# First group of the two 16-head pipelines taken in parts of 1, 1 and 2 tiles

## The chip, the cores and the metric

The kernel runs on one core of one Trainium2 chip. The metric is device time of one launch in microseconds (us): the median of repeated runs. A separate profiled execution gives the trace.

## The reference

A four-layer network with gated cross-attention and mixture-of-experts blocks on `x` of shape (2, 1024, 256), so N = 2048 tokens of 256 numbers, with a context of 64 rows per batch. Everything is float32. Each layer adds two blocks to `x`, each on a layer norm of `x` without learned scale:

```python
x = x + tanh(g_xattn[l]) * xattn_l(layernorm(x), ctx)
x = x + tanh(g_ffn[l])   * ffn_l(layernorm(x))
```

The attention of layers 1 and 3, which the change is about, has 16 heads of width 16 over the 64 context rows of the token's batch:

```python
q, k, v = (split_heads(t @ W + b) for ...)          # queries from x, keys and values from ctx
scores  = einsum('bhqd,bhkd->bhqk', q, k) / sqrt(16)
scores  = where(mask, scores, -1e9)
out     = einsum('bhqk,bhkd->bhqd', softmax(scores), v) @ Wo + bo
```

Layer 0 uses linear attention and a routed feed-forward, layer 2 a single-head attention, layer 1 a dense sum over all eight gated experts, layers 0, 2 and 3 route tokens to experts (one expert per token in layers 0 and 2, two in layer 3, with a capacity in 2 and 3).

## The kernel before

**Tiling.** The residual `x` stays in SBUF as `xs`, 16 tiles of 128 tokens (NT = 16), handled in four groups of four tiles (TG = 4, GW = 512 tokens). Context keys and values of a 16-head layer are turned once into block-diagonal operands `kblk` and `vblk` (`Heads.setup`), so that scores of 16 heads and 64 keys are eight matrix products per tile.

**Stages in order.** Layer 0 attention; layer 0 experts (`moe0`), whose outputs are added by indirect DMA into a copy of the residual in DRAM (`xd`); at its end `heads1.setup` and `xattn2_setup` prepare layers 1 and 2, and `reload(xd)` brings the residual back, one DMA of 512 KB for each group, on SP's queue. Then `middle`: the layer-1 pipeline, the dense experts of layer 1 and the attention of layer 2. Then the experts of layer 2 (`moe_capacity`), which end with `heads3.setup` and another `reload`. Then `last_attention`, the layer-3 pipeline, with the routing of layer 3; then its experts.

**A pipeline.** `Heads.pipeline` walks the 16 tiles. At step i it issues the transposes of the probabilities of tile i-1 (`turned`), the scores and softmax of tile i (`scores`), the products with `vblk` and the division for tile i-1 (`quotients`), and the output product for tile i-2 (`output`), which adds the result to `xs`. Between these it advances two lists of generators: `coming`, which prepares the next group, and `gone`, which norms finished groups for the next block. What a group needs before its scores is made by `ready(g)`: `norm_steps` takes statistics of all four tiles (`stats`, line 203: two VectorE operations per tile, then a handful of operations on 4 elements per partition, with Ln and Exp on ScalarE), normalises two tiles on ScalarE and two on GpSimd (lines 248 and 253), transposes the group with eight TensorE operations (line 271) and copies it out of PSUM on ScalarE (line 179); `query_steps` (line 511) forms the queries of all 512 tokens in two accumulations of two products (line 279), adds the bias on ScalarE (line 517), and adds the gated output bias to the group's rows of `xs` in one GpSimd operation of 128x1024 (line 524). Group 0 runs through all of it first: `run(ready(0))` stands ahead of the loop.

The mask enters the scores as a product that starts the accumulation (line 542); the eight score products are line 548. In layer 1 the softmax subtracts the maximum on VectorE (lines 568 and 569) and takes one exponential (line 578); in layer 3 half of the heads take it one head at a time with the maximum as bias (lines 561 and 564). Line 590 transposes the probabilities, line 609 is `quotients`' product, lines 621 to 625 its division, line 640 the addition to `xs`.

**What sets the order.** The framework records each instruction with its reads and writes, and schedules them when the program is complete: each engine gets its own list, an instruction is placed where its operands are ready by a cost model, and the program's order is the priority. At run time an engine takes its list strictly in order and waits on semaphores. Dependencies go by the region of a tile that an instruction touches.

**Others that the change touches.** `int_ramp` (line 78) makes integer ramps once at the start and converts them. The weights of layer 1's experts come in by SP's queue behind `reload`, and GpSimd forms sums of weight blocks from them (lines 1329 to 1332) while the pipeline runs.

## Time and profile before

| what | value |
|---|---|
| median of 3 runs | 2223.36 us (2222.18 to 2229.72) |
| the profiled execution | 2234.64 us, its span 2232.9 us |
| mean granted TensorE clock in it | 0.941 |
| PE busy | 2070.0 us, 93% of the span |
| DVE, ACT, POOL busy | 1320.5, 934.0, 1148.6 us (59%, 42%, 51%) |
| layer-1 pipeline: reload issued, first statistics, first scores | 338.48, 342.28, 359.25 us |
| layer-3 pipeline: reload issued, first statistics, first scores | 1910.12, 1914.03, 1928.19 us |

PE stands for TensorE's products, PEld for its loads of the stationary operand, DVE for VectorE, ACT for ScalarE, POOL for GpSimd, SP for the engine whose queue issues most DMAs. "Lnnn" is a line of the kernel. Times in the trace count from the first instruction. The granted clock is the share of full speed that TensorE was given; in the stretches shown it is 0.50 or 1.00. Idle time of an engine is written with what released it.

### The profile page before, as it was taken

How to read it: one execution, taken by the hardware profiler on the slowest of the kernel's cores; microseconds unless marked ns; L12 is line 12 of the kernel's file. 1: busy time of each engine (PE TensorE's matmuls, PEld its weight loads, DVE VectorE, ACT ScalarE, POOL GpSimd, SP SyncE). 2: the span in 40 equal slices, each digit the busy share in tenths (PEclk: the TensorE clock that was granted, in tenths of full speed). 3: DMA queues.
4: the chain of work that ended last, by engine and by line, in shares of the span. 5: the costliest groups of instructions: out<-in, count | busy, mean ns of one | idle time of the engine just before them, and what ended most of it. 6: DMA issues, size and time to landing. Idle time of an engine off the chain costs nothing. (4 is left out here: it accounts for less than half of the span.)

```text
span 2232.9 us, 31536 instructions
## 1 busy us (share of the span) xinstructions
PE 2070.0 (93%) x11296; PEld 1739.8 (78%) x11296; DVE 1320.5 (59%) x2920; ACT 934.0 (42%) x2108; POOL 1148.6 (51%) x1341
## 2 busy tenths in 40 slices
PE   6739998999999999999999999999996999698897
PEld 3339995678888788888788887888885999365797
DVE  5851117766666676566666666666564566577564
ACT  4414443653333333333433334333332555374454
POOL 3225655126666556666366665566660665311673
PEclk8859998999999999999999999999995899797899
DMA  3135542012222232222222222322230354111352
GB/s 102 48 105 182 160 138 97 6 43 90 90 85 85 76 102 88 85 85 91 83 91 85 85 86 76 103 86 86 86 104 29 116 140 125 52 39 58 104 149 58
DMA packets 108532, 201.05 MB, mean 90 GB/s; under 512 B 20052, under 2 KB 47960, under 8 KB 105790
## 3 DMA queue, kind: packets, MB, share of 16 engines
q1 hardware_dynamic: 83144, 162.18, 22.7%
q0 software_dynamic: 19728, 36.03, 6.2%
q8 instruction: 90, 1.47, 0.3%
q10 hardware_dynamic: 5504, 0.82, 0.2%
q14 instruction: 66, 0.54, 0.1%
HBM read 206.89 MB, written 21.91 MB: 102 GB/s over the span
## 5 line engine op out<-in xcount | busy, mean ns | idle before, releaser
L1698 PE MATMUL ps_b<-xsum,w 128*128 128x256 f32 x1536 | 386.7, 381 | 2.6 <-DVE c L1724 2.6
L1329 POOL TENSOR_TENSOR w<-w 128x256 f32<-128x256 f32 x224 | 165.0, 737 | 386.2 <-DMA w<-in_L_Wu_dram 184.1
L1698 PEld LDWEIGHTS ps_b<-xsum,w 128*128 128x128 f32 x1536 | 290.7, 190 | 48.5 <-issue 4.6
L1380 ACT COPY u<-ps_b 128x512 f32<-128x512 f32 (+5 forms) x242 | 118.9, 491 | 435.4 <-PE ps_b L1743 255.9
L1698 PE MATMUL ps_a<-hT,w 128*128 128x256 f32 x1024 | 265.9, 381 | 0.2 <-ACT ps_b L1362 0.2
L1698 PEld LDWEIGHTS ps_a<-hT,w 128*128 128x128 f32 x1024 | 194.4, 191 | 27.2 <-ACT ps_b L1362 0.6
L1332 POOL TENSOR_TENSOR w<-w 128x256 f32<-128x256 f32 x224 | 186.0, 830 | 16.9
L1330 POOL TENSOR_TENSOR w<-w 128x256 f32<-128x256 f32 x224 | 193.6, 864 | 0.0
L1331 POOL TENSOR_TENSOR w<-w 128x256 f32<-128x256 f32 x224 | 192.0, 857 | 0.0
L1362 ACT COPY ps_b<-ps_a 128x512 f32<-128x512 f32 (+5 forms) x242 | 115.4, 477 | 121.0 <-DVE b L1728 70.3
L1368 ACT COPY m<-ps_e 128x512 f32<-128x512 f32 (+5 forms) x242 | 117.9, 488 | 39.0 <-PE ps_e L1743 26.4
L1760 POOL TENSOR_TENSOR m<-m,accT 128x256 f32<-128x256 f32 x60 | 71.7, 1196 | 120.4 <-ACT m L1368 118.3
L1698 PE MATMUL ps_e<-hT,w 128*128 128x256 f32 x512 | 133.1, 381 | 0.4 <-ACT m L1368 0.4
L1698 PE MATMUL ps_e<-xsum,w 128*128 128x256 f32 x512 | 132.9, 380 | 0.0
L1724 DVE TENSOR_TENSOR c<-ps_e,u 128x512 f32<-128x512 f32 x64 | 44.2, 691 | 148.7 <-ACT u L1380 148.7
L1743 PE MATMUL ps_b<-t,w 128*128 128x256 f32 x512 | 132.1, 381 | 0.0
L1743 PE MATMUL ps_a<-b,w 128*128 128x256 f32 x512 | 131.4, 379 | 0.0
L1725 DVE TENSOR_TENSOR b<-b,c 128x512 f32<-128x512 f32 x128 | 118.1, 922 | 4.1
L1698 PEld LDWEIGHTS ps_e<-hT,w 128*128 128x128 f32 x512 | 97.4, 191 | 15.5 <-ACT m L1368 1.8
L1705 ACT ACTIVATE b<-b 128x512 f32<-128x512 f32 x128 | 80.7, 631 | 67.9 <-DVE b L1713 62.6
L1743 PEld LDWEIGHTS ps_b<-t,w 128*128 128x128 f32 x512 | 97.7, 191 | 13.3
L1698 PEld LDWEIGHTS ps_e<-xsum,w 128*128 128x128 f32 x512 | 96.7, 190 | 14.1 <-issue 1.3
(418 smaller groups left out, 4413.1 us busy)
## 6 DMA issues: line engine op xcount, KB each, us to landing
w<-in_L_Wg_dram SPq DMA_DIRECT2D x64, 512.0 KB, 3.8
w<-in_L_Wu_dram SPq DMA_DIRECT2D x64, 512.0 KB, 3.8
w<-in_L_Wd_dram SPq DMA_DIRECT2D x64, 512.0 KB, 3.6
w<-in_L_W_dram SPq DMA_DIRECT2D x64, 512.0 KB, 4.2
hd_L<-h SPq DMA_DIRECT2D x8, 512.0 KB, 3.0
b<-b2d SPq DMA_DIRECT2D x23, 128.0 KB, 4.3
xs<-in_x_dram SPq DMA_DIRECT2D x4, 512.0 KB
xd<-xs SPq DMA_DIRECT2D x4, 512.0 KB, 2.8
```

The source lines that it names most:

```text
L1329: lambda: eng.tensor_add(s[0], a21, a22),
L1330: lambda: eng.tensor_sub(s[1], s[0], a11),
L1331: lambda: eng.tensor_sub(s[2], a11, a21),
L1332: lambda: eng.tensor_sub(s[3], a12, s[1]),
L1362: A.copy(self.b, self.pa)
L1368: A.copy(self.sb5, self.pe)
L1380: A.copy(u2, self.b)
L1698: T.matmul(ps[:, q * 256 : (q + 1) * 256], lhsT=lhs[kind][:, q, :], rhs=xr[kind], start=(first and q == 0), stop=True, skip_group_check=True,)
L1705: done[0] = A.activation(dst, src, AF.Silu)
L1725: V.tensor_mul(m[name], m[name], c)
L1743: T.matmul(ps, lhsT=wd[kind][:, q, :], rhs=m["rhs"][kind][:, q * 256 : (q + 1) * 256], start=(clear and q == 0), stop=True, skip_group_che ...
L1760: G.tensor_add(sb, sb, acc[:, i, j])
```

## The change

Group 0 of both 16-head pipelines is taken in parts of one, one and two tiles.

- `reload` brings group 0 back in three DMAs (128, 128 and 256 KB), groups 1 to 3 in one each as before.
- A new `parts_steps` takes statistics, normalises, transposes and copies out one part at a time. The first tile of a part is normalised on ScalarE, the second on GpSimd: in all three tiles on ScalarE and one on GpSimd. A part of n tiles has 2n transposes into one PSUM tile and one copy.
- `query_steps` is split into `new_queries` and `some_queries`, which forms the queries of the given tiles alone and adds the output bias tile by tile, in operations of 128x256, for all groups.
- `Heads.first` runs group 0: four products of the first loaded tile with itself (128x128 by 256 columns) into a PSUM tile that nobody reads, then the parts.
- `pipeline` starts the first part ahead of the scores of tile 0, the second after them, the third after the scores of tile 1; the transposes of tile 0's probabilities come after that. Later groups are prepared as before.
- `int_ramp` keeps its integers in a work buffer (`w`) rather than in one of its own. `stats` uses tiles cut to its n. The router has a parts variant and a tag argument, which nothing calls or sets.

```diff
     def int_ramp(shape, pattern, base, mult, name):
-        ti = const.tile(shape, I32, name=name + "_i")
+        ti = wpool.tile([P, 2048], F32, name="w")[:, : shape[1]].bitcast(I32)
...
+    def parts_steps(g, parts, psp, hpool, hTpool):
+        xg = xs[:, g * TG : (g + 1) * TG, :]
+        h = hpool.tile([P, TG, D], F32, name="h")
+        hT = hTpool.tile([P, NC, GW], F32, name="hT")
+        yield h, hT
+        for t0, n in parts:
+            mv, rstd = stats(xg[:, t0 : t0 + n], n, True)
+            off = small.tile([P, TG], F32, name="off")[:, :n]
+            V.scalar_tensor_tensor(off, mv[:, :, 0], -1.0, rstd, ALU.mult, ALU.mult)
+            for t in range(n):
+                if t % 2:
+                    G.tensor_scalar(
+                        h[:, t0 + t, :], xg[:, t0 + t, :], rstd[:, t : t + 1],
+                        off[:, t : t + 1], ALU.mult, ALU.add,
+                    )
+                else:
+                    A.activation(
+                        h[:, t0 + t, :], xg[:, t0 + t, :], AF.Identity,
+                        bias=off[:, t : t + 1], scale=rstd[:, t : t + 1],
+                    )
+            yield
+            ps = psp.tile([P, GW], F32, name="ps_tr")
+            for c in range(NC):
+                for t in range(n):
+                    T.transpose(
+                        ps[:, (c * n + t) * P : (c * n + t + 1) * P],
+                        h[:, t0 + t, c * P : (c + 1) * P], ident,
+                    )
+            A.copy(
+                hT[:, :, t0 * P : (t0 + n) * P],
+                ps[:, : NC * n * P].rearrange("p (c q) -> p c q", c=NC),
+            )
+            yield t0, n
...
+        def some_queries(self, g, hT, qT, t0, n, pools):
+            at = slice(t0 * P, (t0 + n) * P)
             for c in range(NC):
-                ps = py.tile([P, 512], F32, name="ps_y")
-                mm256(ps, lambda k: self.wq[:, k, c * P : (c + 1) * P], lambda k: hT[:, k, :])
+                ps = pools["py"].tile([P, 512], F32, name="ps_y")
+                mm256(
+                    ps[:, : n * P], lambda k: self.wq[:, k, c * P : (c + 1) * P],
+                    lambda k: hT[:, k, at],
+                )
                 A.activation(
-                    qT[:, c, :], ps, AF.Identity, bias=cols[:, self.c_bq, c : c + 1]
+                    qT[:, c, at], ps[:, : n * P], AF.Identity,
+                    bias=cols[:, self.c_bq, c : c + 1],
                 )
                 yield
-            self.qT[g] = qT
-
-            xg = xs[:, g * TG : (g + 1) * TG, :]
-            G.tensor_add(xg, xg, self.bo.unsqueeze(1).to_broadcast([P, TG, D]))
+            for t in range(g * TG + t0, g * TG + t0 + n):
+                G.tensor_add(xs[:, t, :], xs[:, t, :], self.bo)
+
+        def first(self, parts, pt, hp, hTp, pools):
+            idle = pools["ps"].tile([P, 512], F32, name="ps_s")
+            for _ in range(4):
+                T.matmul(
+                    idle[:, :D], lhsT=xs[:, 0, :P], rhs=xs[:, 0, :], start=True, stop=True
+                )
+            steps = parts_steps(0, parts, pt, hp, hTp)
+            _, hT = next(steps)
+            qT = self.new_queries(0, pools)
+            for found in steps:
+                if found:
+                    run(self.some_queries(0, hT, qT, *found, pools))
+                    yield
...
-            run(ready(0))
+            begun = ready(0)
...
+                if i == 0:
+                    next(begun)
+                if i > 1 and i - 1 < NT:
                     self.turned(i - 1, pools)
                 if i < NT:
                     self.scores(i, pools)
+                if i <= 1:
+                    next(begun)
+                if i == 1:
+                    self.turned(0, pools)
...
+    PARTS = [(0, 1), (1, 1), (2, 2)]
...
     def reload(xd):
-        for g in range(NG):
+        for a, n in ((0, 1), (1, 1), (2, 2), *((g * TG, TG) for g in range(1, NG))):
             nc.sync.dma_start(
-                residual(g), xd[g * GW : (g + 1) * GW, :].rearrange("(t p) d -> p t d", p=P)
+                xs[:, a : a + n, :],
+                xd[a * P : (a + n) * P, :].rearrange("(t p) d -> p t d", p=P),
             )
...
                 def ready(g):
+                    if g == 0:
+                        return heads1.first(PARTS, pools["pt"], hp, hTp, pools)
+                    return later(g)
```

With `if 0 <= i - 1 < NT` replaced by `if i > 1 and i - 1 < NT`, the step order of tiles from 1 on is as before. The layer-3 `ready` is changed in the same way with `heads3`.

More of the change, by code (lines that the diff above doesn't have):

```diff
@@ L202, in stats @@
     def stats(src, n, by_log=False):
-        st = small.tile([P, TG, 6], F32, name="st")
-        mv = small.tile([P, TG, 2], F32, name="mv")
+        st = small.tile([P, TG, 6], F32, name="st")[:, :n]
+        mv = small.tile([P, TG, 2], F32, name="mv")[:, :n]
         for t in range(n):
@@ L207, in stats @@
             V.bn_aggr(mv[:, t, :], st[:, t, :])
-        ve = small.tile([P, TG], F32, name="ve")
+        ve = small.tile([P, TG], F32, name="ve")[:, :n]
         V.tensor_scalar_add(ve, mv[:, :, 1], EPS)
         if by_log:
-            y = small.tile([P, TG], F32, name="y0")
+            y = small.tile([P, TG], F32, name="y0")[:, :n]
             A.activation(y, ve, AF.Ln)
@@ L215, in stats @@
         else:
-            yi = small.tile([P, TG], I32, name="yi")
+            yi = small.tile([P, TG], I32, name="yi")[:, :n]
             V.tensor_single_scalar(yi, ve.bitcast(I32), 1, ALU.logical_shift_right)
@@ L220, in stats @@
         for i in range(1 if by_log else 3):
-            q = small.tile([P, TG], F32, name="q")
+            q = small.tile([P, TG], F32, name="q")[:, :n]
             V.tensor_mul(q, y, y)
             V.scalar_tensor_tensor(q, q, -0.5, ve, ALU.mult, ALU.mult)
-            rstd = small.tile([P, TG], F32, name=f"rstd{i}")
+            rstd = small.tile([P, TG], F32, name=f"rstd{i}")[:, :n]
             V.scalar_tensor_tensor(rstd, q, 1.5, y, ALU.add, ALU.mult)
@@ L511, in query_steps, with new_queries @@
         def query_steps(self, g, hT, pools):
-            two, py = pools["two"], pools["py"]
-            qT = two.tile([P, NC, GW], F32, name="qT", bufs=pools.get("nq", 1))
-            for c in range(NC):
-                ps = py.tile([P, 512], F32, name="ps_y")
-                mm256(ps, lambda k: self.wq[:, k, c * P : (c + 1) * P], lambda k: hT[:, k, :])
+            yield from self.some_queries(g, hT, self.new_queries(g, pools), 0, TG, pools)
+        def new_queries(self, g, pools):
+            self.qT[g] = pools["two"].tile(
+                [P, NC, GW], F32, name="qT", bufs=pools.get("nq", 1)
+            )
+            return self.qT[g]
+        def some_queries(self, g, hT, qT, t0, n, pools):
+            at = slice(t0 * P, (t0 + n) * P)
+            for c in range(NC):
+                ps = pools["py"].tile([P, 512], F32, name="ps_y")
[3 more added lines that the diff above has]
+                )
                 A.activation(
-                    qT[:, c, :], ps, AF.Identity, bias=cols[:, self.c_bq, c : c + 1]
+                    qT[:, c, at], ps[:, : n * P], AF.Identity,
+                    bias=cols[:, self.c_bq, c : c + 1],
                 )
                 yield
-            self.qT[g] = qT
-            xg = xs[:, g * TG : (g + 1) * TG, :]
-            G.tensor_add(xg, xg, self.bo.unsqueeze(1).to_broadcast([P, TG, D]))
+            for t in range(g * TG + t0, g * TG + t0 + n):
[5 more added lines that the diff above has]
+                    idle[:, :D], lhsT=xs[:, 0, :P], rhs=xs[:, 0, :], start=True, stop=True
+                )
+            steps = parts_steps(0, parts, pt, hp, hTp)
[5 more added lines that the diff above has]
+                    yield
         def scores(self, tt, pools):
@@ L653, in pipeline @@
                 if i < NT and i % TG == 0:
-                    advance(coming, 99)
+                    advance(coming, 999)
                     if i + TG < NT:
                         coming.append(ready(i // TG + 1))
-                if 0 <= i - 1 < NT:
+                if i == 0:
+                    next(begun)
+                if i > 1 and i - 1 < NT:
                     self.turned(i - 1, pools)
@@ L802, in bc, with logit_steps @@
         return ap.unsqueeze(2).to_broadcast([P, ap.shape[1], n])
-    def logit_steps(ps, at, hT, which):
-        for t in range(TG):
+    def logit_steps(ps, at, hT, which, t0=0, n=TG):
+        for t in range(t0, t0 + n):
             mm256(
@@ L812, in logit_steps, with choose_steps @@
                 yield
-    def choose_steps(psp, rp, nt, ps, bias, top, before):
+    def choose_steps(psp, rp, nt, ps, bias, top, before, tag="ps_m"):
         rev = rev8.unsqueeze(1).to_broadcast([P, nt, E])
@@ L850, in choose_steps @@
         W = nt * E
-        pk = psp.tile([P, 512], F32, name="ps_m")
+        pk = psp.tile([P, 512], F32, name=tag)
         T.matmul(pk[:, :W], lhsT=upper_b, rhs=flat, start=True, stop=False)
@@ L857, in choose_steps @@
             )
-        pc = psp.tile([P, 512], F32, name="ps_m")
+        pc = psp.tile([P, 512], F32, name=tag)
         for t in range(nt):
@@ L1243, in group_steps, with parts_steps, slot_steps @@
             yield from self.slot_steps(g * TG, TG, ps, psp, rp)
-        def slot_steps(self, t0, nt, ps, psp, rp):
+        def parts_steps(self, g, parts, pt, psp, hpool, hTpool, rp, tag="ps_m"):
+            steps = parts_steps(g, parts, pt, hpool, hTpool)
+            h, hT = next(steps)
+            lg = rp.tile([P, TG, E], F32, name="r_some")
+            for found in steps:
+                if found:
+                    t0, n = found
+                    ps = psp.tile([P, 512], F32, name=tag)
+                    run(logit_steps(ps, 0, hT, self.which, t0, n))
+                    biased = lg[:, t0 : t0 + n]
+                    at = ps[:, t0 * E : (t0 + n) * E].rearrange("p (t e) -> p t e", e=E)
+                    if self.bias is None:
+                        V.tensor_copy(biased, at)
+                    else:
+                        V.tensor_add(
+                            biased, at, self.bias.unsqueeze(1).to_broadcast([P, n, E])
+                        )
+                yield found
+            self.rows(g, h)
+            yield
+            yield from self.slot_steps(
+                g * TG, TG, lg.rearrange("p t e -> p (t e)"), psp, rp, tag, biased=True
+            )
+        def slot_steps(self, t0, nt, ps, psp, rp, tag="ps_m", biased=False):
             top = self.top
             p1, _, ex, rk = yield from choose_steps(
-                psp, rp, nt, ps, self.bias, top, self.before
+                psp, rp, nt, ps, None if biased else self.bias, top, self.before, tag
             )
@@ L1300, in slot_steps @@
             yield
-            pi = psp.tile([P, 512], F32, name="ps_m")
+            pi = psp.tile([P, 512], F32, name=tag)
             for t in range(n):
@@ L1817, in ready, with later @@
                 def ready(g):
+                    if g == 0:
+                        return heads1.first(PARTS, pools["pt"], hp, hTp, pools)
+                    return later(g)
+                def later(g):
                     _, hT = yield from norm_steps(g, pools["pt"], hp, hTp, by_act=True, halved=True)
@@ L1916, in ready, with later @@
             def ready(g):
+                if g == 0:
+                    return heads3.first(PARTS, pools["pt"], hp, hTp, pools)
+                return later(g)
+            def later(g):
                 _, hT = yield from norm_steps(g, pools["pt"], hp, hTp, by_act=True, halved=True)
```

## The prediction

> **What bounds the kernel now.** First the page: PE is busy for 93% of the span and no other engine for over 59%; its slices of 55.8 us stand mostly at 9; the 8 of the seventh and the 6 of the 35th hold the starts of the two 16-head pipelines. The chain of waits over the whole span is split over hundreds of short pieces, so I went to the two places that the change touches: the start of the layer-1 pipeline (after the reload at 338.5 us) and of the layer-3 pipeline (reload at 1910.1 us). The windows there, cut where the granted clock changes; the columns are the stretch, its length, the busy time of PE, PEld, DVE, ACT and POOL with instruction counts, granted clock, DMA share and GB/s.

> ```profile
> 341.00:349.40 8.40, 6.10 (x24) 4.29 (x23) 3.98 (x19) 0.00 (x0) 0.00 (x0) 0.50 1.07 395
> 349.40:356.20 6.80, 5.41 (x14) 2.67 (x14) 6.76 (x25) 2.80 (x8) 4.71 (x6) 0.50 0.62 245
> 356.20:363.00 6.80, 3.62 (x13) 1.34 (x11) 3.28 (x6) 3.63 (x8) 6.40 (x9) 1.00 0.00 1
> 363.00:366.40 3.40, 3.14 (x13) 1.85 (x13) 2.29 (x4) 0.00 (x0) 3.40 (x5) 0.50 0.00 0
> ...
> 1909.20:1918.70 9.50, 0.00 (x0) 0.00 (x0) 4.67 (x26) 1.12 (x4) 1.18 (x7) 0.50 0.78 275
> 1918.70:1922.90 4.20, 3.98 (x10) 1.93 (x10) 4.13 (x14) 2.08 (x7) 3.40 (x3) 0.50 0.02 5
> 1922.90:1929.70 6.80, 3.99 (x14) 1.78 (x15) 3.65 (x7) 3.30 (x7) 5.70 (x6) 1.00 0.00 0
> 1929.70:1943.40 13.70, 13.70 (x66) 7.85 (x63) 5.23 (x9) 7.66 (x24) 1.42 (x1) 0.50 0.00 1
> ```

> The reader sees two losses: TensorE stands (9.5 us flat in layer 3), and what it does it does mostly at half clock. From 1943.4 and 366.4 on the clock is full and PE is 97% busy (19.40 and 19.61 of 20 us in the windows from 1950 on), so PE's work sets the end of both stages, and what counts is how early that work is done. Then the timeline, for what keeps TensorE waiting (start, length, engine, line, operation, tiles, shapes, count, idle time before and its releaser):

> ```profile
> 342.28 0.43 DVE L206 BATCH_NORM_STATS2 st<-xs 128x6 f32<-128x256 f32 x1 [3.49 <-DMA xs<-xd]
> ...
> 354.60 2.35 POOL L524 TENSOR_TENSOR xs<-xs,bo 128x1024 f32<-128x1024 f32 x1
> 354.70 2.27 DVE L225 SCALAR_TENSOR_TENSOR rstd<-q,y 128x4 f32<-128x4 f32 x1
> ...
> 359.25 0.70 PE L548 MATMUL ps_s<-kblk,qT 64*128 64x256 f32 x4 [0.22 <-ACT qT L517]
> ```

> ```profile
> 1914.03 0.75 DVE L206 BATCH_NORM_STATS2 st<-xs 128x6 f32<-128x256 f32 x2 [5.39 <-DMA xs<-xd_L]
> ...
> 1918.73 2.09 PE L271 MATMUL ps_tr<-ident,h 128*128 128x128 f32 x8 [11.56 <-POOL h L253]
> ...
> 1924.47 2.21 DVE L225 SCALAR_TENSOR_TENSOR rstd<-q,y 128x4 f32<-128x4 f32 x1
> ...
> 1928.19 0.70 PE L548 MATMUL ps_s<-kblk,qT 64*128 64x256 f32 x4 [1.93 <-ACT qT L517]
> ```

> From the landing of group 0 to the first score product 17.0 us pass in layer 1 and 14.2 in layer 3: four tiles of statistics, normalising, eight transposes and the 512-column queries, all before tile 0 gets its scores. Three times (354.70, 1919.54, 1924.47) a 4-element DVE operation of some 0.15 us takes 2.1 to 2.3 us beside the 2.35 us bias add of POOL.

> **The change part by part.** *Reload in six DMAs.* Layer 3 issues at 1910.12 and moves 131 KB in 1911 to 1912 and 276 KB in the next us; the first 512 KB are through at about 1913.3, and DVE starts 0.7 later. The first 128 KB are through at 1912.0: tile 0 lands at about 1912.7, 1.3 us earlier; in layer 1, by its windows in the same way, at 341.0 and not 342.3. Two more issues of 0.5 us each on SP put groups 1 to 3, and the weight loads queued behind them, 1.0 us later; the queue moves 380 to 390 GB/s without a break until 353 and its end is not waited for, so I cost this at nothing; without that cover, 1.0 us.

> *Tile 0 alone.* Its chain from rows of layer 3: statistics 0.40+0.16+0.15 on DVE (0.65 with overlap), two ACT steps 0.6, the four small DVE steps 1.15 with other tiles' statistics between (1916.80 to 1917.95), ACT's normalising 0.65, two transposes at half clock 0.7, the copy of 256 elements 0.5 (512 take 0.59), two 128-column queries 0.6, two bias steps 0.75 (512 take 0.67 each): 5.6 us. Scores could begin at 1912.7+5.6 = 1918.3, not 1928.2. This is not the gain: afterwards PE is the bound.

> *What it is worth at the end.* I count PE's work in us of full clock, busy times clock. Layer 3, landing to 1943.4: 3.98/2 + 3.99 + 13.70/2 = 12.8. Layer 1, from 341.0 to 366.4: 6.10/2 + 5.41/2 + 3.62 + 3.14/2 = 10.9, the layer-2 setup included. The same work has to be done after. The clock steps at 339.1, 356.2, 363.0, 366.4 and at 1909.2, 1922.9, 1929.7, 1943.4, always whole multiples of 3.41 us apart, so the new ramp gets a full clock at one of these edges. [...]

> Layer 3: PE begins real work at about 1916.2 and, with tiles coming singly, is taken to be 80% occupied (between the 59% of 1922.9 to 1929.7 and the full 13.70 after). At half clock until 1929.7 it does 13.5*0.4 = 5.4; the other 7.4 at 95% take 7.8: done at 1937.5, 5.9 us earlier. Full clock one edge sooner (1926.3) gives 7.9, one later (1933.1) 3.9. I take 5.9, because the 13.7 us after 1929.7, transposes and half-row scores at 100% busy, show that this mix does not raise the clock soon. Layer 1: the setup products keep PE at 85%; half clock until 356.2 does 6.5, the rest 4.5 takes 4.7: done at 360.9, 5.5 earlier (7.4 with the edge at 352.8, 3.6 with 359.6).

> *Four unread products.* No row shows one; a 256-column fp32 pass at half clock starts every 0.42 us (1929.85 to 1931.12), so four take 1.7. In layer 3 PE has nothing else (11.56 idle); in layer 1 they stand on its in-order queue with the setup behind them: between -1.7 (the clock rises an edge sooner) and +1.7 a head. I take 0.

> *Bias by tiles.* Sixteen adds a stage at 0.73 (the 128x256 sums) and not four at 2.35: POOL +2.3 us a stage, idle afterwards in layer 3. DVE behind one waits 0.7 and not 2.2; the hits at 354.70, 1919.54 and 1924.47 lie in the stretches counted above, so nothing is added. [...] The first rival has a row that waited longer.

> *The rest.* Eight more query products and loads a head at about 0.1 over the same columns, 0.5 in all on PE at worst for both; ACT gets one more tile and some ten short steps a head, under scores that wait for PE. The ramps in work buffers are read at 9.85 to 10.46, the buffers next written at 24.5: nothing. The parts variant of the router and the new arguments are not called: nothing. `pipeline` turns tile 0 after the scores of tile 1: one exchange, nothing.

> Sum: -5.9-5.5+0.5 = -10.9. The profiled execution took 2234.64 (span 2232.9 and 1.7 around it), so 2223.7 by its own time; the median is 11.3 below that execution, and 2223.4-10.9 = 2212.5. About 0.3%, 6.7 us, is what a measurement of this kernel can tell from no change.

> **The rivals.** *POOL's train takes layer 1's gain back.* POOL runs weight sums almost without a break from 351.5 to 378.8. In that run one operation waited through seven sums:

> ```profile
> 373.29 4.91 DVE L625 SCALAR_TENSOR_TENSOR oT<-rs,oT 128x256 f32<-128x256 f32 x1
> ```

> Tile 0 now reaches L625 some 10 us deeper in the run; if it gets through only at its end, the first output product is no earlier than its 378.3 of now and layer 1 gains nothing: -5.4, 2218. Against it: the other small DVE steps there waited for one sum each. *The clock is raised at once.* If the four products fill enough of a window, layer 3 runs full from 1916.1: 10 us at 80%, the other 4.8 at 95%, done at 1931.3, 12.1 earlier; with layer 1's 7.4 that is -19, 2204. [...] 1.7 us of queries and four transposes sufficed in 1919.5 to 1922.9; 1.9 of mask products did not in 349.4 to 352.8. *The clock stays down (slower).* The pieces are sparser than the dense 512-column queries that raised it at 356.2 and 1922.9; each further edge at half clock costs 3.41/2 = 1.7. It decides from 10.9/1.7, over six edges more than I count in the two ramps together; ten give +6 to +7, 2230. For it: four edges in a row at full occupancy after 1929.7. [...] Against it: group 1's 512-column queries must come within some 20 us. *It does not do what it says:* where the parts are queued in order behind other groups' steps on ACT and DVE, as the normalising of groups 1 and 2 was put ahead of tile 0's scores before, tile 0 is not early: -1, 2222.

> **How the numbers follow.** Forecast 0.55 (its own range 2206 to 2219: an edge sooner or later in both layers gives 2209 to 2216, and the products' bounds some 3 more); POOL's train 0.18; clock at once 0.12; not what it says 0.07; clock down 0.08. Faster: 0.55 + 0.12 + a sixth of the train's 0.18 = 0.70; the train's rest and the 0.07 are same, 0.22; slower 0.08. The range takes in the first three down to the clock-at-once case and up to the fourth, and leaves out the clock-down case and the tails of those two: 2203 to 2222.

> **What would show it.** First statistics within 3 us of the reload's first issue; scores of tile 0 at about 6 us after that landing; PE idle before the first transposes of layer 3 some 2.5 us shorter; the windows from the landing to the steady 97% shorter by 5 to 6 us in each layer, with the clock full for good by about 20 us after the landing; no DVE step of 2.2 us beside a bias add. It is wrong if scores of tile 0 still start over 12 us after the landing, if the first output of layer 1 waits for POOL's last sum, or if the half clock lasts as long as before.

## The result and the profile after

| | before | after |
|---|---|---|
| median of the timed runs | 2224.43 us (2220.96 to 2231.23, 10 runs) | 2212.22 us (2204.32 to 2220.75, 10 runs) |
| ratio (that of the two medians is 0.9945, inside the interval) | | 0.9931, 95% interval 0.9914 to 0.9948 |
| profiled execution, span, mean granted clock | 2234.64, 2232.9 us, 0.941 | 2211.2, 2209.5 us, 0.955 |
| layer 1, from the reload's first issue: statistics, scores, first and last output product | 3.8, 20.8, 39.9, 127.2 us | 2.0, 11.4, 32.2, 120.6 us |
| layer 3, the same | 3.9, 18.1, 39.8, 140.8 us | 2.1, 9.3, 32.7, 133.1 us |
| half clock in the first 60 us after the issue, layers 1 and 3 | 20.5 and 26.4 us | 3.2 and 10.2 us |

The change takes off 12.2 us by the medians. In the two profiles the stages, from the reload's first issue to the last output product, are 6.6 and 7.7 us shorter; the rest of the two spans, which the change hardly touches, differs by 9.1 us more. That is put down to the scatter of single executions: the runs of before in this study went from 2211.5 to 2237.1 us, and its profiled one, at 2234.6, is 10 us above its median. So the profiles show where time went, and the timed runs how much it was. "Head" below is the first part of such a stage, 60 us where it is counted.

The windows of the changed kernel at the two starts, cut where the clock steps. Columns: stretch, length, busy time of PE, PEld, DVE, ACT and POOL, granted clock, DMA share, GB/s.

```profile
334.60:337.80 3.20, 3.20 (x13) 1.93 (x13) 1.46 (x6) 0.00 (x0) 0.00 (x0) 0.51 0.59 176
337.80:347.00 9.20, 7.84 (x49) 5.64 (x48) 8.09 (x47) 3.54 (x13) 3.16 (x5) 1.00 1.03 364
347.00:356.50 9.50, 8.39 (x58) 5.98 (x58) 8.99 (x17) 6.98 (x16) 9.50 (x16) 1.00 0.38 143
...
1894.20:1901.00 6.80, 5.93 (x16) 3.88 (x16) 5.07 (x28) 2.20 (x8) 1.40 (x2) 0.50 0.99 321
1901.00:1911.30 10.30, 6.49 (x43) 4.34 (x44) 8.30 (x31) 8.17 (x32) 5.53 (x8) 1.00 0.10 38
1911.30:1914.70 3.40, 3.40 (x9) 2.46 (x9) 1.11 (x2) 2.57 (x6) 3.21 (x6) 0.50 0.01 2
1914.70:1934.70 20.00, 19.84 (x211) 12.81 (x209) 11.34 (x31) 13.35 (x38) 1.75 (x3) 1.00 0.00 1
```

Where the layer-3 head had 13.70 us in one piece at half clock, fully busy, it now has 3.40; where TensorE stood for 11.56 us ahead of its first transposes, it now stands for 3.76 and is then busy for 5.93 of 6.80 (3.78 of it the unread products). In layer 1 the clock is full from 337.8 on. The timeline of the same kernel, the lines that answer to the waits shown of before:

```profile
341.16 1.97 PE L578 MATMUL ps_s<-xs 128*128 128x256 f32 x8
...
345.99 0.70 PE L611 MATMUL ps_s<-kblk,qT 64*128 64x256 f32 x4
...
349.79 0.56 POOL L279 TENSOR_SCALAR h<-xs,rstd,off 128x256 f32<-128x256 f32 x1
...
1895.02 0.43 DVE L206 BATCH_NORM_STATS2 st<-xs 128x6 f32<-128x256 f32 x1 [2.32 <-DMA xs<-xd_L]
...
1895.04 3.78 PE L578 MATMUL ps_s<-xs 128*128 128x256 f32 x8 [3.76 <-DMA xs<-xd_L]
...
1902.17 1.15 PE L611 MATMUL ps_s<-kblk,qT 64*128 64x256 f32 x8
```

The two stages as a whole, layers 1 and 3, before and then after, in the columns of the windows above:

```profile
338.48:465.70 127.22, 117.47 (x999) 75.66 (x1000) 96.82 (x246) 67.50 (x132) 33.72 (x42) 0.92 0.12 45
1910.12:2050.90 140.78, 123.07 (x1037) 80.56 (x1038) 94.46 (x328) 85.66 (x264) 22.97 (x35) 0.86 0.12 42
```

```profile
334.59:455.20 120.61, 114.23 (x1026) 75.89 (x1025) 93.73 (x257) 69.88 (x142) 35.36 (x53) 0.99 0.13 47
1892.89:2026.00 133.11, 121.05 (x1064) 82.54 (x1065) 92.41 (x338) 87.51 (x274) 24.15 (x46) 0.92 0.13 45
```

Length less PE's busy time is the time that TensorE stood: 27.46 us before, 18.44 after. Of its busy time 45.3 us were at half clock before and 23.8 after; counted at half, they cost 10.8 us less. Its work, counted at full clock, rose by 5.5 us. So the 14.3 us in these two profiles are 9.0 of less standing and 10.8 of less half-clock work, less 5.5 of added work.

The four unread products are eight records (each product of this size shows as two) and take 3.78 us at half clock, 1.97 at full. Scores follow at 345.99 and 1902.17. The 0.56 us at 349.79, GpSimd's normalising of group 0's fourth tile ("tile 3" below), will matter.

### The profile page after: what moved, and what is told of

Its sections match the earlier page's. It is cut to its first block, busy times and chain, and to the rows that moved or that the text cites. A ratio compares the mean times of both kernels' runs of the same rounds, so it can differ in the third digit from the quotient of the medians.

```text
span 2209.5 us, 31694 instructions
## 1 busy us (share of the span) xinstructions
PE 2055.3 (93%) x11344; PEld 1735.2 (79%) x11344; DVE 1313.8 (59%) x2940; ACT 938.3 (42%) x2128; POOL 1150.2 (52%) x1363
## 4 chain that ended last, share of the span: by engine, by line
PE 79%; DVE 8%; DMA 4%; POOL 3%; ACT 3%; issue 3%; POOLq 0%; SPq 0%; ACTq 0%; DVEq 0%
PE ps_b L1796 15%; PE ps_e L1796 10%; PE ps_a L1796 10%; PE ps_b L1841 7%; PE ps_m L315 6%; PE ps_a L1841 5%; PE ps_e L1841 4%; PE ps_y L1051 4%; PE ps_y L315 3%; PE ps_b L1637 2%; PE ps_b L1664 2%; PE ps_a L1637 2%; PE ps_e L1637 1%; PE ps_e L1664 1%; PE ps_a L1664 1%
## 5 line engine op out<-in xcount | busy, mean ns | idle before, releaser
L1796 PEld LDWEIGHTS ps_a<-hT,w 128*128 128x128 f32 x1024 | 193.6, 190 | 26.4
L1430 POOL TENSOR_TENSOR w<-w 128x256 f32<-128x256 f32 x224 | 186.5, 833 | 17.1
```

What stands on the lines that cost most here:

```text
L1430: lambda: eng.tensor_sub(s[3], a12, s[1]),
L1796: T.matmul(ps[:, q * 256 : (q + 1) * 256], lhsT=lhs[kind][:, q, :], rhs=xr[kind], start=(first and q == 0), stop=True, skip_group_check=True,)
```

## The experiments

Twelve kernels, in three sets; in each set they were timed against the same runs of the kernel before. "The changed kernel" is the one whose result stands above. Theory A: tile 0's early scores make the gain. Theory B: the unread products make it, by raising the clock. Theory C: the bias by tiles makes it. Theories D, E and F came up on the way and are stated where they were put to the test.

For all of them, the table. "Half clock, all" is the mean over a kernel's timed runs of 2 x (1 - granted clock) x span; "half clock, heads" is read in the one profile, the first 60 us after each of the two reloads, added. The last column is the mean time less half of "half clock, all": what the runs would take if all half-clock time were half as long.

| kernel | median us | ratio (95%) | half clock, all | half clock, heads | time less half |
|---|---|---|---|---|---|
| before (92 runs in three sets) | 2225.5 to 2227.2 | 1 | 236 to 239 | 46.9 | 2107.5 to 2107.9 |
| changed kernel | 2212.2 | 0.9931 (0.9914 to 0.9948) | 208.7 | 13.4 | 2108.2 |
| no_products | 2226.7 | 1.0004 (0.9983 to 1.0026) | 230.0 | 29.3 | 2111.9 |
| whole_group | 2220.0 | 0.9958 (0.9939 to 0.9978) | 220.3 | 17.1 | 2108.7 |
| whole_bias | 2212.8 | 0.9945 (0.9923 to 0.9966) | 207.9 | 13.6 | 2109.6 |
| one_load | 2219.2 | 0.9947 (0.9924 to 0.9970) | 217.6 | 30.8 | 2108.7 |
| products_only | 2224.1 | 1.0002 (0.9982 to 1.0023) | 231.5 | 37.6 | 2108.1 |
| thin_products | 2215.6 | 0.9946 (0.9923 to 0.9970) | 217.7 | 22.7 | 2106.6 |
| no_products_act | 2212.9 | 0.9950 (0.9931 to 0.9968) | 208.6 | 15.7 | 2108.7 |
| early | 2217.4 | 0.9958 (0.9941 to 0.9976) | 205.9 | 13.4 | 2112.9 |
| tile3_act | 2216.2 | 0.9956 (0.9932 to 0.9979) | 211.8 | 17.0 | 2109.8 |
| parts_only | 2224.7 | 0.9994 (0.9967 to 1.0021) | 229.0 | 38.9 | 2109.7 |
| loads_bias | 2221.3 | 0.9985 (0.9962 to 1.0007) | 221.3 | 32.4 | 2111.3 |
| all_act | 2213.8 | 0.9937 (0.9912 to 0.9962) | 204.9 | 9.9 | 2110.1 |

Two columns carry the main reading. The last one hardly moves: 2106.6 to 2112.9 in every kernel, while the times move by 14 us. And "heads" and "all" move together: from before to the changed kernel 33.5 us less in the heads and 28 to 30 less in all; for products_only 9 and 6, for parts_only 8 and 9, for all_act 37 and 33 (one profile stands for a kernel in the heads' column; those of no_products, one_load and loads_bias fit less well). So what these kernels gain is, within 5 us, half of the half-clock time that they lose: 14 to 15 us for the changed kernel, beside 12.2 by the medians and some 15 by the ratio. That most of it goes at the two starts rests on the two columns moving together; in the two profiles alone, some 30 us of half clock differ outside the heads too. And the last column does not tell slow work from standing, since TensorE also stands in half-clock time: in the two stages above the standing fell by nearly as much as the clock's cost, and the added work hid it in the sum. With that said, the question is which part of the change takes the half clock away.

**no_products**: the four products left out.

```diff
-            idle = pools["ps"].tile([P, 512], F32, name="ps_s")
-            for _ in range(4):
-                T.matmul(
-                    idle[:, :D], lhsT=xs[:, 0, :P], rhs=xs[:, 0, :], start=True, stop=True
-                )
```

> The changed kernel without its four unread products; all else kept. Stage lengths below run from the first issue of the reload to the last output product of the pipeline: 127.0 and 140.3 us in the kernel before (layers 1 and 3), 120.4 and 132.7 in the changed one. Theory A (the early scores of tile 0 pay; the products are a side matter): within 3 us of the changed kernel, 2211 to 2215; layer 3's clock full at most one edge (3.4 us) later, its length 132 to 135; layer 1 119 to 121, since there the products take 2.0 us of TensorE in the middle of the setup. Theory B (the products raise the clock and that is the gain): 2217 or more, layer 3 at 137 or more, with the half clock lasting past 13 us after the reload, as before.

Measured 1.0004: the whole gain is gone, although scores came as early (12.9 and 8.2 us after the reload). The time spoke for theory B and against A as it stood, but B also has layer 3 at 137 us or more, and it took 134.4. The first output product of layer 1 came at 40.7 us and not at 32.2, and the profile shows a wait ahead of it. First the timeline, then the windows of 3.41 us around it:

```profile
360.99 0.72 POOL L1424 TENSOR_TENSOR w<-w 128x256 f32<-128x256 f32 x1
361.67 0.72 POOL L1423 TENSOR_TENSOR w<-w 128x256 f32<-128x256 f32 x1
362.37 0.56 POOL L279 TENSOR_SCALAR h<-xs,rstd,off 128x256 f32<-128x256 f32 x1
```

```profile
362.98 0.90 PE L292 MATMUL ps_tr<-ident,h 128*128 128x128 f32 x3 [5.07 <-POOL h L279]
```

```profile
354.08:357.49 3.41, 1.87 (x10) 0.88 (x10) 3.41 (x8) 1.95 (x4) 3.41 (x7) 1.00 0.10 40
357.49:360.90 3.41, 0.33 (x1) 0.14 (x1) 1.37 (x4) 0.04 (x1) 3.33 (x6) 1.00 0.00 0
360.90:364.31 3.41, 1.33 (x6) 1.33 (x7) 0.00 (x0) 0.39 (x1) 3.41 (x7) 0.50 0.01 2
```

Tile 3's normalising stands behind a row of weight sums in GpSimd's list: it runs 23.9 us after the reload, against 15.2 in the changed kernel. TensorE waits 5.07 us for it at 362.98; the window 357.49 to 360.90 holds 0.33 us of its work, and the next one begins at half clock. No code that orders GpSimd was edited: taking the products out moved the order that the scheduler wrote, since it places instructions by its own estimate of when operands are ready. So two things had changed, TensorE's early work and the order (theory D: the order lost the gain).

**whole_group**: group 0 normed and given its queries at once; the products, three loads and bias by tiles kept.

```diff
-            steps = parts_steps(0, parts, pt, hp, hTp)
-            _, hT = next(steps)
...
+            _, hT = norm_group(0, pt, hp, hTp, by_act=True, halved=True)
+            self.queries(0, hT, pools)
+            yield
```

> The changed kernel with group 0 normed, transposed and queried as a whole again, ahead of the loop; the four products, the three loads and the bias by tiles stay. Theory A (early scores pay): most of the gain is gone, 2219 to 2224, layers 1 and 3 at 124 to 127 and 137 to 140, scores of tile 0 again over 12 us after the landing. Theory B (clock): the products still raise it, 2212 to 2216. Theory C (the bias by tiles unblocks VectorE): 2212 to 2217, and no 4-element VectorE step over 1 us in the head.

0.9958, 2220.0: some 60% of the gain stays without the parts, though the time is in theory A's range. Scores came at 15.6 and 13.1 us, and half clock in the heads was 17.1 us.

**whole_bias**: the output bias added by groups, as before.

```diff
-            for t in range(g * TG + t0, g * TG + t0 + n):
-                G.tensor_add(xs[:, t, :], xs[:, t, :], self.bo)
+            if t0 + n == TG:
+                xg = xs[:, g * TG : (g + 1) * TG, :]
+                G.tensor_add(xg, xg, self.bo.unsqueeze(1).to_broadcast([P, TG, D]))
```

> The changed kernel with the output bias added for a whole group at once (128x1024 on GpSimd, for group 0 after its third part). Theory A: 2211 to 2215, both stages within 1.5 us of the changed kernel; VectorE steps of 2.2 us return but TensorE has other work by then. Theory C (bias by tiles is what pays): 2217 or more, with the stages 3 us or more longer each.

0.9945, its interval around the changed kernel's 0.9931: with the other three parts there, this one is worth nothing that shows. Theory C falls.

**one_load**: group 0 loaded by one DMA.

```diff
-        for a, n in ((0, 1), (1, 1), (2, 2), *((g * TG, TG) for g in range(1, NG))):
+        for a, n in ((g * TG, TG) for g in range(NG)):
```

> The changed kernel with one 512 KB load for group 0 again. Theory A: the chain of tile 0 starts 1.3 to 1.7 us later in each layer (first statistics 3.8 us after the first issue and not 2.1), and the end follows by 1 to 1.7 a layer: 2213 to 2216. Rival (TensorE is behind anyway, the landing is hidden): 2211 to 2213, stages unchanged within 0.5 us.

0.9947: by the ratio the same, though the median of 2219.2 lies above both expectations (before had 2227.2 in this set). Its one profile took 2228 us beside a median of 2219, with 30.8 us of half clock in the heads, so it is judged by the runs alone, and these do not settle whether the loads are worth some us.

**products_only**: the kernel before, with the four products ahead of `run(ready(0))`.

```diff
+            idle = pools["ps"].tile([P, 512], F32, name="ps_s")
+            for _ in range(4):
+                T.matmul(
+                    idle[:, :D], lhsT=xs[:, 0, :P], rhs=xs[:, 0, :], start=True, stop=True
+                )
             run(ready(0))
```

> The kernel before with one thing added: the four unread 256-column products of tile 0 ahead of each pipeline's first group; loads, norm, queries and bias add as before. Theory A (the gain is tile 0's early scores): the scores still begin 18 to 21 us after the reload, nothing is gained: 2222 to 2228. Theory B (the gain is less time at half clock, and the products bring it): time at half clock falls from 239 us to 210 to 220 us over the run and the time to 2213 to 2217, with the scores as late as before.

1.0002: nothing. Theory B falls in its plain form. The windows of its layer-3 head show what became of their early work:

```profile
1899.70:1906.50 6.80, 3.00 (x7) 2.46 (x8) 3.02 (x17) 0.41 (x2) 0.00 (x0) 0.50 0.84 281
1906.50:1916.80 10.30, 6.84 (x25) 2.93 (x24) 9.45 (x28) 5.00 (x13) 8.16 (x7) 1.00 0.18 70
1916.80:1930.40 13.60, 12.45 (x62) 7.41 (x63) 3.96 (x6) 7.53 (x25) 2.95 (x3) 0.50 0.00 1
```

The clock does rise early, at 1906.5. But TensorE then works for 6.84 of 10.30 us, the clock falls again, and 13.6 us at half clock follow, as before. So raising the clock early was worth nothing here. Standing behind the rise is not the whole reason: the changed kernel worked for no more of its 10.30 us (6.49, from 1901.0), lost the clock too, and had it back after 3.40 us. What the two profiles differ in is how long the clock then stayed down, and why isn't shown.

**thin_products**: the four products cut from 256 columns to 32.

```diff
-                    idle[:, :D], lhsT=xs[:, 0, :P], rhs=xs[:, 0, :], start=True, stop=True
+                    idle[:, :32], lhsT=xs[:, 0, :P], rhs=xs[:, 0, :32], start=True, stop=True
```

> The changed kernel with the four products cut from 256 columns to 32, in the same place: the order of the work is kept, the heat is an eighth. Theory B: half clock 225 to 232 us and 2219 to 2224, though the first output of layer 1 comes early. Theory D (what the kernel without products lost is the place of tile 3's normalising in GpSimd's queue, and the clock only follows from that): half clock 205 to 212 us and 2211 to 2214, as with whole products.

0.9946, with tile 3's normalising at 15.4 us as in the changed kernel: the gain is there, or nearly (3 us more by the medians, inside both intervals). An eighth of the columns was not an eighth of the time: the thin products take 1.06 us in layer 1 and 1.67 in layer 3, against 1.97 and 3.78. Time and half clock lie between the two expectations, nearer to D's. The one profile took 2224.1 us beside a median of 2215.6, and layer 1 had lost its gain in it: the first output product came at 40.8 us. A VectorE step for a later group's norm was held for 9.03 us beside GpSimd's weight sums (shown in the last section); VectorE's chain behind it ended at 363.76 with the `off` that ScalarE's normalising reads, and that began at 363.84 (its row names a weight sum that ended at 363.74); behind it stood the copy that TensorE waited 5.52 us for:

```profile
363.84 1.09 ACT L248 ACTIVATE h<-xs,off,rstd 128x256 f32<-128x256 f32 x2 [5.81 <-POOL w L1427]
```

```profile
365.72 2.08 PE L315 MATMUL ps_y<-hT,wq 128*128 128x512 f32 x2 [5.52 <-ACT hT L179]
```

So the gain of layer 1 can be lost in two ways with GpSimd's sums: by an operation's place among them, and by what they hold up on VectorE.

**no_products_act**: no products, and all four tiles of group 0 normalised on ScalarE, so that none can stand behind the weight sums.

```diff
-                if t % 2:
-                    G.tensor_scalar(
-                        h[:, t0 + t, :], xg[:, t0 + t, :], rstd[:, t : t + 1],
...
+                A.activation(
+                    h[:, t0 + t, :], xg[:, t0 + t, :], AF.Identity,
+                    bias=off[:, t : t + 1], scale=rstd[:, t : t + 1],
+                )
```

> The changed kernel without the four products, and with all four tiles of group 0 normalised on ScalarE, so that none of them can stand behind GpSimd's weight sums. Theory B: half clock stays at 225 to 232 us, but time less half of the half clock goes back from 2112 to about 2108: 2220 to 2224. Theory D: the half clock falls too, to 205 to 212, and the time to 2211 to 2214.

0.9950, half clock 208.6 us, as with the products (208.7), in six runs. The products aren't needed for the gain, which is theory D.

**early**: eight more unread products, of tables long in place, ahead of the four.

```diff
+            late = self.vblk[:, B - 1].rearrange("p i j d -> p (i j d)")
+            for _ in range(8):
+                T.matmul(
+                    idle[:, :D], lhsT=late[:, :P], rhs=self.wq[:, 0, :], start=True, stop=True
+                )
```

> The changed kernel with eight more unread 256-column products ahead of the four, of tables that are long in place, so that TensorE has work while the first tile is on its way. Theory B: the clock is full an edge or more earlier in layer 3, half clock 195 to 207 us and 2205 to 2211. If the place of the products in the window decides less than their being ahead of the first tile (no further gain): 2211 to 2214; if they only delay the first transposes: over 2214.

2217.4, a miss in time for all but the last of the three expectations. The half clock was no less than in the changed kernel (205.9 against 208.7), and time less half rose by 4.7 us. In layer 1 the first score product came at 17.9 us and not at 11.4: the added products stood ahead of tile 0 on TensorE's list and took 4.25 us there, and in this profile the setup before them ran at half clock.

**tile3_act**: no products, tile 3 alone moved to ScalarE (`if t0 + t == 1` in place of `if t % 2`).

> The changed kernel without the four products, with tile 3 of group 0 normalised on ScalarE and tile 1 left on GpSimd. Theory D (without products the gain was lost because tile 3's normalising stands behind nine weight sums on GpSimd in layer 1): the first output of layer 1 comes at 32 to 35 us, half clock 205 to 215 us, 2211 to 2216. Theory E (it was tile 1, or something that both tiles changed together): 2220 to 2227.

0.9956, 2216.2: most of the gain is back, with the first output of layer 1 at 33.8 us. Moving one 0.56 us operation out of another engine's list went with some 10 us (2226.7 against 2216.2). The wait of 5.07 us is the one that went. It isn't shown that it makes all of the 10 us: the list of TensorE differs a little as well between the two (mask products and transposes exchanged), and in the two profiles layer 3, which had no such wait, is shorter by as much as layer 1 (134.4 to 126.9 us, beside 128.7 to 121.5).

**parts_only**: the parts of 1, 1 and 2 tiles alone, all normalised on ScalarE; one load, bias by groups, no products.

> Only the norm and queries of group 0 in parts of 1, 1 and 2 tiles, all four normalised on ScalarE; one load a group, the bias added by groups, no unread products. Theory A (early scores let TensorE be busy, and so at full clock, earlier): scores at 10 to 13 us after the reload, half clock 208 to 218 us, 2212 to 2217. Theory F (the gain is a sum of small things of all parts): under half of the gain, 2219 to 2224.

0.9994: nothing, though layer 3's first scores came at 10.3 us. So theory A isn't the whole either. The windows of its layer-3 head, and a line of the timeline in the second of them:

```profile
1907.60:1919.70 12.10, 4.97 (x20) 3.55 (x20) 7.70 (x47) 5.07 (x17) 1.51 (x3) 0.50 0.65 217
1919.70:1923.10 3.40, 1.79 (x13) 1.33 (x11) 3.40 (x3) 1.29 (x5) 3.40 (x2) 1.00 0.00 0
1923.10:1933.40 10.30, 8.75 (x24) 4.75 (x23) 5.94 (x11) 6.12 (x22) 2.45 (x3) 0.50 0.01 2
```

```profile
1919.62 2.31 DVE L209 TENSOR_SCALAR ve<-mv 128x4 f32<-128x4 f32 x1
...
1922.18 2.56 DVE L1420 TENSOR_TENSOR w<-w 128x256 f32<-128x256 f32 x1
```

The clock rose for one window only. In it VectorE spent its 3.40 us on three operations, two of which waited beside GpSimd's bias add by groups; TensorE had 1.79 us of work, and 10.3 us at half clock followed.

**loads_bias**: three loads and bias by tiles, without parts and products.

> The rest without that: three loads for group 0 and the bias by tiles, group 0 normed and given its queries at once, no unread products. Theory A: scores at 16 to 20 us and the time near that of before, 2222 to 2227; the kernel with whole group and products (2220.0) then owed its part to the products' heat ahead of dense 512-column queries. Theory F: about 2219 to 2221.

0.9985 with an interval from 0.9962 to 1.0007: between nothing and some half of the gain. It tells A from F badly.

**all_act**: the whole changed kernel, all four tiles of group 0 on ScalarE; meant to beat it.

> The whole changed kernel, products included, with all four tiles of group 0 normalised on ScalarE: a candidate to beat it. Theory A: nothing waits for GpSimd ahead of tile 0 to 3, scores as early, half clock 200 to 210 us, 2209 to 2213. If ScalarE's two more tiles delay the evictions of the first queries and exponentials: 2214 to 2218.

0.9937 (0.9912 to 0.9962) beside 0.9931: it has the least half clock of all (204.9 us), but it is not faster than the changed kernel by any difference that these runs can tell.

What follows: theories A, B and C, each as a single cause, fall, and the parts don't add up. Bias by tiles or the loads can go alone at little cost, and so can the products if nothing stands in GpSimd's way; parts alone, and products alone, give nothing. What sets the kernels with the gain apart stays open. It is not that TensorE never stands for most of a window at the start of a stage: the changed kernel has such a window itself, 15 us after layer 3's reload,

```profile
1907.88:1911.29 3.41, 1.18 (x9) 0.99 (x10) 3.38 (x11) 2.66 (x12) 3.41 (x5) 1.00 0.00 0
```

and loses the clock behind it, for one window. Which of loads and bias parts_only lacked was not tried, the table's small differences (thin_products to whole_bias) lie inside the intervals, and with one profile for a kernel, whose runs differ by 10 to 26 us, the heads can't be compared kernel by kernel.

## Why the prediction was right, and where it wasn't

The time (2212.5 forecast, 2212.2 measured) and the two terms that make it held: layer 3 was to be 5.9 us shorter and is 7.7, layer 1 5.5 and is 6.6, in single profiles. That the time is met within 0.3 us is luck. What was right is that TensorE's work sets the end of a stage, and that the half clock of its first 20 us is a large part of what delays it; some of the terms behind the two numbers were wrong and nearly cancelled. Point by point:

- *The landing*, 1.3 us earlier: the first statistics came 1.8 us earlier in both layers (3.80 to 2.04, 3.91 to 2.13).
- *Tile 0's chain*, 5.6 us from the landing to the scores: 9.4 in layer 1 and 7.2 in layer 3. In layer 3 the unread products stand ahead of it: with thin_products it was 6.1. In layer 1 they stand behind setup work on TensorE's list and run at 341.16, 4.5 us after the first statistics (336.6); the chain was costed from layer 3 without that. The step was called "not the gain", and parts_only bears that out.
- *What it is worth at the end*: near in size by two errors of opposite sign. Layer 3 was to run at half clock until some 17 us after the landing and then stay full; it got full clock 6 us after the landing, lost it for one window (1911.3 to 1914.7) and had it for good at 19.7 us. Layer 1 was to get it 15 us after the landing and got it 1.1 us after. The forecast's steps have TensorE working 13.0 and 10.8 us at half clock after the landing in layers 1 and 3; it was 1.1 and 9.3, which is worth 6.7 us more than forecast. Against that, "the same work has to be done after" failed: it rose by 5.5 us in the two stages, where 0.5 stood in the sum. The rest is in how long TensorE stood.
- *Layer 1's early clock* is not the rival of the clock raised at once, since the unread products ran at 341.16 and the clock had risen at 337.7. The window ahead of the rise, 334.3 to 337.7, was full of setup products (3.40 us); the one of before, 339.1 to 342.5, held 2.38. In the profiles of the other kernels the half clock around the reload ended anywhere from 2.2 us after it (thin_products) to 16.6 (parts_only), and in tile3_act and whole_group the clock was full there throughout. How much of it the change made, and how much the place of the clock's windows in that execution, isn't shown.
- *Four unread products*, "four take 1.7" at half clock: 3.78, since each shows as two records 0.43 us apart, and one was counted. They are 3.9 us of the 5.5 of added work. The value "I take 0" holds for the time (no_products_act has the gain without them, products_only has none with them), but the step failed in what it looked at. Their presence also decided where the scheduler put tile 3's normalising, and in the kernel that only left them out the whole gain was gone. A bound of 1.7 us a head for an instruction that nobody reads was drawn from its duration alone.
- *Bias by tiles*, 0: whole_bias agrees. Its cover is the rest of the change: in parts_only, where adds by groups were back together with other parts, two VectorE operations of 2.31 and 2.56 us lie in the window that lost the clock.
- *The rest*, +0.5: the added work without the unread products is 1.6 us in the two profiles.

Of the rivals, *POOL's train* did starve VectorE in the changed kernel, at another operation than the one named. TensorE then waited 1.79 us for a copy (at 361.01), and little was taken back (first output 32.2 us after the reload, 39.9 before):

```profile
354.75 3.85 DVE L245 SCALAR_TENSOR_TENSOR off<-mv,rstd 128x4 f32<-128x4 f32 x1
```

Where the train did take layer 1's gain back, it was in no_products by an operation's place in GpSimd's own list, and in the profile of thin_products by holding VectorE, as the rival has it, again at another operation. So the rival was real, and whether it strikes is decided by small things. *The clock raised at once*: not by the products in layer 1, as said; in layer 3 the clock was full 6 us after the landing, but not for good. *The clock stays down*: not so in the changed kernel; products_only and parts_only show it, each without gain, neither slower. *Does not do what it says*: no.

## What to carry to other kernels

Where the granted clock of an engine changes within a run, as it does here between 0.50 and 1.00, set the half-clock time of the timed runs beside each kernel's time: here the two went together over fourteen kernels (the time less half of it stayed within 2106.6 to 2112.9 us), whatever part of the change was in or out. Before a gain is put down to the clock, split the stage into standing, work at full clock and what the half clock costs: here all three moved. A clock that was up early bought nothing by itself (products_only, up at 1906.5: 1.0002). With a scheduler between the code and the engines' lists, compare the lists before crediting an effect to what was added or removed: here taking out four products that nobody reads lost the whole gain, and the wait that came with it was for another engine's operation, which had moved in its list.

## What the runs showed of the hardware

**VectorE beside GpSimd.** A 4-element VectorE operation of thin_products was held for 9.03 us. GpSimd's operations around it:

```profile
353.24 9.03 DVE L222 TENSOR_TENSOR q<-y 128x4 f32<-128x4 f32 x1
```

```profile
360.84 0.73 POOL L1429 TENSOR_TENSOR w<-w 128x256 f32<-128x256 f32 x1
361.52 0.73 POOL L1428 TENSOR_TENSOR w<-w 128x256 f32<-128x256 f32 x1
362.33 0.73 POOL L1430 TENSOR_TENSOR w<-w 128x256 f32<-128x256 f32 x1
```

From 353.32 to 362.25 one GpSimd addition starts every 0.69 us (the last of four bias adds, then twelve weight sums), before the last has ended by the profile's spans, and the VectorE operation ends at 362.27, in the 0.08 us in which GpSimd stood. The 3.85 us case in the changed kernel ends the same way: at 358.60, between a sum that ends at 358.58 and the next at 358.66. Pauses of 0.08 us between two weight sums stand in no_products (359.55 to 359.63) and in before (361.09 to 361.17) as well. So the operation of 9.03 us lasted through twelve sums, and ended when GpSimd paused.
